# An involution and two ternary convolutions: three of seven neighbourhood columns transposed from SBUF instead of through DRAM

## The chip, the core and the metric

The kernel runs on one core of a Trainium2 chip. The metric is the device time of one execution in microseconds. Before the change three runs gave 2461.24, 2463.05 and 2464.96 us; the median is 2463.05 us. The profile comes from one further execution, whose span is 2469.9 us.

## The reference

The input x is float32 with 8 images, 256 channels and 56 x 56 positions. Two layers follow each other, and only the first is touched here.

```python
# layer 0, an involution with 7x7 taps and 16 groups of 16 channels
ker = einsum('bchw,oc->bohw', gn(x), w_reduce) + b_reduce        # 256 -> 64
ker = einsum('bchw,oc->bohw', ker, w_span) + b_span              # 64 -> 49*16
out = (ker.reshape(B, G, 1, 49, H, W) * patches(gn(x))).sum(axis=3)
x = x + out
# layer 1: two 3x3 convolutions with ternary weights, batch norms, relu
x = x + block(gn(x))
```

`gn` is a group norm with 32 groups. For each position and each group of 16 channels the involution makes 49 weights out of the 256 channels at that position, and sums the 7 x 7 neighbourhood (padded with zeros) with those weights. The ternary weights of the second layer depend on the mean, maximum and minimum of each whole weight tensor.

## The kernel before, in words

**Layout.** An image is worked on in four quarters (`NCQ`) of 64 channels. A quarter lies in SBUF as a tile `x` with 128 partitions: 64 channels of the upper half of the image (28 rows), then the same 64 channels of the lower half. The image is cut into tiles of 3 x 8 positions (`PY`, `PX`): ten tile rows (`TY`) in each half, the last with one row of positions, and seven tile columns (`TX`). The neighbourhood of a tile is 9 x 14 = 126 positions (`NQ`).

**The involution as matmuls.** For each tile and each group there is a matrix of 126 neighbours by 24 positions. TensorE makes these matrices from the reduced tensor `kr` and the slid weights `wl` (`generate`, line 606): 14 units for a quarter, each in one PSUM tile `pg` of two banks, that ACT (L631) and DVE (L636) move with the bias into the SBUF tile `a`. A unit has four to eight pixels' worth of matmuls; the ACT part of a unit comes first, and DVE's write to `a` waits for it. `apply_row` (line 646) then multiplies, for each tile row, the 126 neighbours by 128 channels (`q`) with the matrices: 28 small matmuls into one PSUM bank `pa` (L660). `pick_out` (line 666) takes the right half of each product out with ACT (L672) and DVE (L673) into `inv`, and POOL adds it to `x` in place (L676).

**The neighbourhoods.** `q` holds the neighbours on the partitions, so the normalised image must be transposed. `prep` (line 542) does this in strips of seven image rows: POOL normalises a strip and copies each tile column with its margin of three into `xn` (L565; three instructions for `PLACES`), TensorE transposes the seven columns into a PSUM tile `pt` (L571), ACT copies `pt` to `stg` (L574), and SP stores `stg` to a DRAM scratch `xtd` (L556, from the list `tasks`, two a row by `transfer`). `load_q` (line 592) reads for each tile row the 126 lines that it needs, 441 KB with all seven columns, four rows ahead (`NQB`, `prefetch`).

**The order of the work.** The main loop (lines 762 to 800) runs over 32 quarters of ten rows. A row issues, in this order: a store or load of x, two stores of strips, `apply_row`, the prefetch of a q, small statistics on DVE, `pick_out`, one or two units of the next quarter's `generate` (`PER_ROW`), and every row from the 24th of an image on one half step of `prep` for the next image (32 half steps, into row 15 of the next image). `pin` keeps each engine's instructions in the order of the text. Ahead of the loop stands a start that a scheduler orders: the first image's loads, `params` and `reduce`, `prep(0)`, the quantising of w1 and w2 (`quantize`, line 176, on DVE with one matmul for the sum, L201), and `generate` for the first quarter. The q buffers take their place in SBUF from the memory of the quantiser, so the first q loads wait for its last store.

**PSUM.** Eight banks: `ps_p` has three tiles of two banks, shared by `pg`, `pt`, the tiles `pk` of `reduce` (L524) and all small sums; `ps_a` has two banks for `pa`.

After the loop come two convolution phases (`conv_phase`) and a final pass. No line of theirs is changed.

Of the kernel before, what the change touches and what calls it, by code (L numbers as in the profile page):

```python
# [7 lines left out]
F32 = mybir.dt.float32  # L8
F32R = mybir.dt.float32r
AF = mybir.ActivationFunctionType  # L10
ALU = mybir.AluOpType
AX = mybir.AxisListType
PSUM = bass.MemoryType.PSUM
DRAM = bass.MemoryType.DRAM

P = 128
# [26 lines left out]

HQ = TY * PY + K - 1
RP = TX * P
SR = HH // 4
NSP = SR * QX

# [3 lines left out]

PER_ROW = (2, 1, 2, 1, 2, 1, 2, 1, 2, 0)
NQB = 4

NCB = 4
NC = NHW // NCB
# [14 lines left out]
@with_exitstack  # L74
def involution_tri_block_kernel(
    ctx: ExitStack, tc: tile.TileContext,
    x, w_red, b_red, w_line, b_tile, w1, w2, g1, b1, g2, b2, grp, ident, half, out,
):
    nc = tc.nc
    out = out.rearrange("b c h w -> b c (h w)")  # L80
# [348 lines left out]


    with ExitStack() as ph1:
        ps_p = ph1.enter_context(tc.tile_pool(name="ps_p", bufs=3, space=PSUM))
        ps_a = ph1.enter_context(tc.tile_pool(name="ps_a", bufs=2, space=PSUM))

        def ps_tile(name):
# [2 lines left out]
        def ps_flat(name):  # L438
            return ps_tile(name).rearrange("p a f -> p (a f)")

        xpool = ph1.enter_context(tc.tile_pool(name="xpool", bufs=2 * NCQ))
        fix = ph1.enter_context(tc.tile_pool(name="fix", bufs=1))
        work = ph1.enter_context(tc.tile_pool(name="work", bufs=2))

# [17 lines left out]
        def params(b):  # L462


            dst = small.tile([P, NCQ, 2], F32, tag="gn1", name=f"gn1_{b}")
            yield from group_norm_params(mvs.pop(b), dst, ps_flat, f"a{b}")
            ps = ps_flat(f"br_{b}")
            for c in range(NCQ):
                nc.vector.tensor_scalar(
                    wrn[:, c, :].rearrange("p (i r) -> p i r", i=2),  # L470
                    wr[:, c, :].unsqueeze(1).to_broadcast([P, 2, CR]),
                    dst[:, c, 0:1], None, ALU.mult)
                for i in range(2):
                    nc.tensor.matmul(ps[i * CR:(i + 1) * CR, :1], wr[:CH, c, :], dst[:CH, c, 1:2],
                                     start=(c == 0), stop=(c == NCQ - 1))
            prm[b] = dst
            yield
            nc.vector.tensor_tensor(brn, br, ps[:, :1], ALU.add)

        gst1, mvs = {}, {}  # L480
        prm, xs = {}, {}
        for c in range(NCQ):
            for j in range(2):
                load_x(0, c, j)
# [15 lines left out]
        bt = fixed([NQ, NCQ, GQ, NP], "bt", b_tile)  # L500
        kr = [fixed([P, PX, NT + (NE if py == 0 else 0)], f"kr{py}") for py in range(PY)]

        xn = fixed([P, TX, SR, QX], "xn")
        nc.gpsimd.memset(xn, 0.0)
        zero = xn.rearrange("p k r x -> p (k r x)")

        for d in (d for ds in xt_d for d in ds):
# [29 lines left out]

        PLACES = ((PAD, 0, PX), (0, PX - PAD, PAD), (PAD + PX, 0, PAD))  # L540

        def prep(b):

            for c in range(NCQ):
                d = xt_d[b % 2][c][:]

                def store(src, row, o=None, d=d):

                    n = src.shape[0]
                    if o is None:
                        src, to = src.rearrange("p k c -> p (k c)"), [[1, RP]]
                    else:
                        to = [[P, TX], [1, CH]]
                    nc.sync.dma_start(  # L556
                        bass.AP(d.tensor, d.offset + row * QX * RP + (o or 0), [[RP, n]] + to), src)

                for s in range(HH // SR):
                    xv = xs[b, c][:, s * SR * W:(s + 1) * SR * W].rearrange(  # L560
                        "p (r k j) -> p k r j", k=TX, j=PX)
                    for k, (x0, j0, n) in enumerate(PLACES):
                        to, fr = ((slice(0, TX), slice(0, TX)), (slice(1, TX), slice(0, TX - 1)),
                                  (slice(0, TX - 1), slice(1, TX)))[k]
                        nc.gpsimd.tensor_scalar(  # L565
                            xn[:, to, :, x0:x0 + n], xv[:, fr, :, j0:j0 + n],
                            prm[b][:, c, 0:1], prm[b][:, c, 1:2], ALU.mult, ALU.add)
                    yield
                    pt = ps_flat(f"pt_{b}_{c}_{s}")
                    for k in range(TX):  # L570
                        nc.tensor.transpose(pt[:NSP, k * P:(k + 1) * P],  # L571
                                            xn[:, k].rearrange("p r x -> p (r x)"), ident_sb)
                    stg = work.tile([P, TX, P], F32, tag="stg", name=f"stg_{b}_{c}_{s}")
                    nc.scalar.copy(stg[:NSP].rearrange("p k c -> p (k c)"), pt[:NSP, :RP])  # L574
                    tasks.append(lambda stg=stg, s=s: store(stg[:NSP], PAD + s * SR))

                    e = PAD * QX
                    if s == 0:
                        tasks.append(lambda stg=stg: store(stg[:e, :, CH:], PAD + HH, 0))
                    elif s == HH // SR - 1:  # L580
                        tasks.append(lambda stg=stg: store(stg[NSP - e:NSP, :, :CH], 0, CH))
                    yield
# [9 lines left out]
        def load_q(b, c, ty):  # L592

            q = qpool.tile([P, TX, P], F32, tag="q", name=f"q_{b}_{c}_{ty}")
            d = xt_d[b % 2][c][:]
            src = bass.AP(d.tensor, d.offset + PY * ty * QX * RP, [[RP, NQ], [1, RP]])
            nc.sync.dma_start(q[:NQ].rearrange("p k c -> p (k c)"), src)
            return q

        def views(a):  # L600

# [150 lines left out]
        quarters = [(b, c) for b in range(B) for c in range(NCQ)]  # L752


        X_AT = (0, 1, 4, 5, 7, 8, 10, 11)
        STRIPS_AT = 23
        for _ in range(NQB):
            prefetch()
        pin(start=True)
        last = None  # L760
        strips = iter(())
        for m, (b, c) in enumerate(quarters):
            a = a_next
            gen = iter(())
            if m + 1 < len(quarters):
                a_next = matrices(m + 1)
                gen = generate(*quarters[m + 1], a_next)
            more = b + 1 < B
            for ty in range(TY):
                r = c * TY + ty  # L770

                if last is not None and ty in (2, 3):
                    store_x1(*last, ty - 2)
                elif more and r in X_AT:
                    load_x(b + 1, X_AT.index(r) // 2, X_AT.index(r) % 2)
                transfer(2)

                row = apply_row(b, c, a, ty)
                prefetch()

                if more and r >= 20:
                    if r == 20:
                        norm = params(b + 1)
                    next(norm, None)
                if ty == 1 and last is not None:
                    gn2_stats(*last, TY)
                elif ty >= 2:
                    gn2_stats(b, c, ty - 1)
                if more and 4 <= r < 20:
                    gn1_stats(b + 1, (r - 4) // NCB, (r - 4) % NCB)  # L790
                pick_out(b, c, ty, *row)
                for _ in range(PER_ROW[ty]):
                    next(gen, None)
                if more and r == STRIPS_AT:
                    strips = prep(b + 1)
                next(strips, None)
                pin()
            for _ in gen:
                pass
# [107 lines left out]
```

## Time and profile before

| stretch, us | what runs | us | TensorE busy | TensorE clock | DMA share |
|---|---|---|---|---|---|
| 0 to 205 | start: first image, quantiser, first quarter's matrices | 205 | 63.1 | 0.64 | 0.40 |
| 206 to 1305 | loop over the quarters | 1099 | 908.6 | 0.92 | 0.72 |
| 1305 to 2220 | two convolution phases | 915 | 857.2 | 0.97, 0.96 | 0.34, 0.33 |
| 2220 to 2470 | final pass | 250 | 0 | 0.50 | 0.97 |

"TensorE busy" is the time in which at least one of its matmuls is under way. The clock is the share of full speed that the core was granted; 0.50 is the half clock in which TensorE stands when it has little to do. The DMA share is the mean busy share of the core's 16 DMA engines. In an idle column of the profile, "<-" names what ended a wait; "issue" stands where no semaphore ended it.

The largest DMA kinds of the loop are the q loads (441 KB each, 320 of them in the kernel), the strip stores (343 KB, 128), and the loads and stores of x (392 KB, 64 each).

### The profile page before, as it was taken

Reading aid. Unit: us, or ns where it says so; the run is one execution under the profiler, and the core shown is the slowest. Engines: PE = TensorE matmul, PEld = TensorE weight load, DVE = VectorE, ACT = ScalarE, POOL = GpSimd, SP = SyncE. Lnnn points to the kernel's source line nnn. Section 1 sums busy time; section 2 is a strip of 40 time slices with the busy share of each in tenths; the row PEclk is TensorE's granted clock in tenths of the full one; section 3 lists DMA queues with packets and bytes.
Section 4 is the critical chain, followed back from the end, with each engine's and each line's share of the span. In section 5 each row is a group of like instructions: output and inputs, shape, how many; then the busy total and the mean of one; then the engine's idle time right before and its main releaser. Section 6 shows DMA issues by size and latency. Waiting matters only on the chain.

```text
span 2469.9 us, 69728 instructions
## 1 busy us (share of the span) xinstructions
PE 1830.0 (74%) x30504; PEld 1700.9 (69%) x30504; DVE 1668.2 (68%) x2554; ACT 1171.8 (47%) x2084; POOL 381.7 (15%) x747
## 2 busy tenths in 40 slices
PE   3515878879787887878876999999499999980000
PEld 2315767768676776767766999999499999980000
DVE  4375656465555646455557999999499999974444
ACT  1202443445444353444433766676356667654433
POOL 1301232333323232332421000000000000000000
PEclk8557998899899898999997999999799999995555
DMA  5228587686858677585775332332423323329998
GB/s 173 89 115 271 167 253 207 209 236 196 255 168 249 202 222 231 176 257 172 234 220 194 130 136 107 117 146 83 183 89 142 116 107 143 123 84 429 428 429 373
DMA packets 127739, 485.44 MB, mean 197 GB/s; under 512 B 33102, under 2 KB 35532, under 8 KB 118732
## 3 DMA queue, kind: packets, MB, share of 16 engines
q1 hardware_dynamic: 121120, 440.03, 52.7%
q10 hardware_dynamic: 6316, 40.97, 4.0%
q8 instruction: 240, 3.93, 0.7%
q14 instruction: 63, 0.52, 0.1%
HBM read 315.76 MB, written 165.18 MB: 195 GB/s over the span
## 4 chain that ended last, share of the span: by engine, by line
PE 66%; DMA 13%; issue 10%; DVE 7%; POOL 2%; ACT 2%; ACTq 0%; SPq 0%; POOLq 0%; DVEq 0%
PE c L384 35%; PE pg L627 15%; PE pa L660 8%; PE pt L571 5%; DMA y1f<-y1d 4%; DMA out_y<-x1f 3%; PE pk L524 2%; DVE a L636 2%; POOL xn L565 1%; DVE x1f L845 1%; DMA x1f<-x1d 1%; ACT a L631 1%; DMA y2f<-y2d 1%; DMA w_w<-in_w 1%; DMA q<-xtd 1%
## 5 line engine op out<-in xcount | busy, mean ns | idle before, releaser
L384 PE MATMUL c<-pl,wq 128*128 128x392 f32 x4608 | 855.9, 348 | 50.3 <-ACT pl L290 32.4
L384 PEld LDWEIGHTS c<-pl,wq 128*128 128x128 f32 x4608 | 853.9, 189 | 52.1 <-ACT pl L290 33.2
L636 DVE TENSOR_TENSOR a<-pg,bt 126x756 f32<-126x756 f32 (+3 forms) x640 | 393.1, 657 | 296.1 <-ACT a L631 256.3
L627 PE MATMUL pg<-kr,wl 64*126 64x140 f32 (+1 forms) x6144 | 485.5, 306 | 78.1 <-issue 54.5
L627 PEld LDWEIGHTS pg<-kr,wl 64*126 64x126 f32 x6144 | 420.7, 207 | 103.1 <-issue 79.5
L660 PE MATMUL pa<-a,q 126*32 126x48 f32 x17920 | 282.9, 212 | 151.6 <-issue 84.7
L660 PEld LDWEIGHTS pa<-a,q 126*32 126x32 f32 x17920 | 233.5, 115 | 208.2 <-issue 168.4
L631 ACT ACTIVATE a<-pg,bt 126x126 f32<-126x126 f32 x768 | 242.7, 475 | 242.7 <-PE pg L627 242.7
L676 POOL TENSOR_TENSOR x<-x,inv 128x168 f32<-128x168 f32 x320 | 166.0, 519 | 800.0 <-DVE inv L673 783.6
L672 ACT ACTIVATE inv<-pa,half_sb 128x168 f32<-128x168 f32 x320 | 126.1, 394 | 298.2 <-PE pa L660 283.4
L673 DVE SCALAR_TENSOR_TENSOR inv<-pa,half_sb,inv 128x168 f32<-128x168 f32 x320 | 118.7, 371 | 195.4 <-ACT inv L672 193.7
L290 ACT CAST pl<-r 128x812 fp32r<-128x812 f32 x192 | 162.5, 867 | 153.9 <-DVE r L285 136.7
L565 POOL TENSOR_SCALAR xn<-x,gn 128x126 f32<-128x126 f32 (+1 forms) x384 | 205.3, 558 | 63.1 <-DMA xtd<-xn 34.0
L347 ACT ACTIVATE dummy<-y,nc 128x1568 f32<-128x1568 f32 x128 | 205.4, 1605 | 15.6 <-DVE y L370 14.3
L291 DVE TENSOR_TENSOR pl<-r,pl 128x812 fp32r<-128x812 f32 x192 | 186.9, 1002 | 30.3 <-ACT pl L290 29.4
L574 ACT COPY stg<-pt 98x896 f32<-98x896 f32 x128 | 117.0, 914 | 159.0 <-PE pt L571 114.6
L571 PE MATMUL pt<-ident_sb,xn 128*98 128x128 f32 x896 | 148.0, 308 | 48.2 <-POOL xn L565 39.3
L571 PEld LDWEIGHTS pt<-ident_sb,xn 128*98 128x98 f32 x896 | 105.8, 141 | 79.4 <-POOL xn L565 55.3
L135 DVE BATCH_NORM_STATS2 st<-x 128x6 f32<-128x392 f32 x256 | 138.1, 556 | 10.3 <-DMA x<-in_x 9.9
L271 POOL MEMSET xp<- 128x116 f32 x32 | 6.3, 196 | 817.0 <-DVE a L285 816.9
L826 ACT ACTIVATE xp<-raw,bi_bn,sc_bn 128x392 f32<-128x392 f32 (+1 forms) x128 | 84.8, 720 | 71.7 <-DVE a L285 57.1
L816 ACT ACTIVATE xp<-raw,gn 128x392 f32<-128x392 f32 (+1 forms) x128 | 85.2, 721 | 56.7 <-DVE a L285 50.9
(127 smaller groups left out, 1362.0 us busy)
## 6 DMA issues: line engine op xcount, KB each, us to landing
q<-xtd SPq DMA_DIRECT2D x320, 441.0 KB
xtd<-stg SPq DMA_DIRECT2D x128, 343.0 KB
raw<-x1d SPq DMA_DIRECT2D x32, 812.0 KB
raw<-y1d SPq DMA_DIRECT2D x32, 812.0 KB
x<-in_x SPq DMA_DIRECT2D x64, 392.0 KB
x1d<-x SPq DMA_DIRECT2D x64, 392.0 KB
y1d<-y SPq DMA_DIRECT2D x32, 784.0 KB
y2d<-y SPq DMA_DIRECT2D x32, 784.0 KB
```

The lines of the kernel that those rows point to most:

```text
L135: nc.vector.bn_stats(st[:, j, :], xt[:, j * NC:(j + 1) * NC])
L290: nc.scalar.copy(hi, r)
L291: nc.vector.tensor_tensor(lo, r, hi.bitcast(F32), ALU.subtract)
L347: nc.scalar.activation(dummy, y[:, to], f, bias=shift[:, to:to + 1], accum_out=stats[:, to, j, n:n + 1])
L384: nc.tensor.matmul(ps[:, to, :NM], wq[:, k, t, dx, to * P:(to + 1) * P], part[:, t, :, dx:dx + W], start=(c == 0), stop=(c == last))
L565: nc.gpsimd.tensor_scalar(xn[:, to, :, x0:x0 + n], xv[:, fr, :, j0:j0 + n], prm[b][:, c, 0:1], prm[b][:, c, 1:2], ALU.mult, ALU.add)
L571: nc.tensor.transpose(pt[:NSP, k * P:(k + 1) * P], xn[:, k].rearrange("p r x -> p (r x)"), ident_sb)
L627: nc.tensor.matmul(dst, wl[rows, c, gp, o:o + NQ], kr[py][rows, px, :], start=True, stop=True)
L631: nc.scalar.activation(whole[:, g0 + i, p0 + j], ps[:NQ, i, j * nt:(j + 1) * nt], AF.Identity, bias=bt[:, c, g0 + i, p0 + j:p0 + j + 1])
L636: nc.vector.tensor_tensor(dst[:, g0:g0 + 2, p0:p0 + nv].rearrange("q g p t -> q g t p"), ps[:NQ, :, t0 * nv:t1 * nv].rearrange("q i (t p) ...
L660: nc.tensor.matmul(ps[o:o + 32, k * 2 * n:(k + 1) * 2 * n], q[:NQ, k, o:o + 32], av[:, t + k, g * 2 * n:(g + 1) * 2 * n], start=True, stop ...
L676: nc.gpsimd.tensor_tensor(xv, xv, iv.rearrange("p t (y x) -> p y t x", x=PX), ALU.add)
```

## The change

Tile columns 0 to 3 (`NK` = 4) keep the way through DRAM. Columns 4 to 6 (`NX` = 3) get their neighbourhoods on the chip:

- `surround(b, c)` builds for one quarter a tile `xe` (3 columns x 34 rows x 14 positions on 128 partitions, two of them, zeroed once): POOL normalises the quarter in four parts of seven rows, and in one more part the three rows above and below each half. Those six rows come from a new input `x_around` by a load of 168 KB; `side` turns the shift of the norm off where the rows lie outside the image. One part is issued in every second row (even `ty`), for the next quarter.
- `transpose_q(b, c, ty)` transposes the three columns of a tile row into a PSUM bank `pt` and lets ACT copy them into the free part of that row's `q`. In the loop it stands right after `apply_row` and the prefetch, for the row two ahead (`QLEAD`).
- `xn`, `stg`, the scratch `xtd` and the DMAs on them shrink from seven columns to four.
- PSUM: `ps_p` goes from three tiles to two; the strips' transposes leave it and share two new banks `pt` of the pool `ps_a` with `transpose_q`.
- `x` has seven buffers instead of eight, and the load of an image's fourth quarter moves from rows 10 and 11 to rows 14 and 15.

```diff
+NK = 4
+NX = TX - NK
 HQ = TY * PY + K - 1
-RP = TX * P
+RP = NK * P
+QLEAD = 2
...
-        ps_p = ph1.enter_context(tc.tile_pool(name="ps_p", bufs=3, space=PSUM))
+        ps_p = ph1.enter_context(tc.tile_pool(name="ps_p", bufs=2, space=PSUM))
...
-        xpool = ph1.enter_context(tc.tile_pool(name="xpool", bufs=2 * NCQ))
+        xpool = ph1.enter_context(tc.tile_pool(name="xpool", bufs=2 * NCQ - 1))
...
-        xn = fixed([P, TX, SR, QX], "xn")
+        xn = fixed([P, NK, SR, QX], "xn")
+        xe = [fixed([P, NX, HQ, QX], f"xe{i}") for i in range(2)]
...
+        def surround(b, c):
+            dst, p = xe[c % 2], prm[b]
+            around = work.tile([P, 2, PAD * W], F32, tag="xa", name=f"xa_{b}_{c}")
+            nc.sync.dma_start(around.rearrange("p s f -> p (s f)"), x_around[b, c])
+            for part in (0, 1, None, 2, 3):
+                if part is None:
+                    for j, r0 in enumerate((0, PAD + HH)):
+                        spread(dst[:, :, r0:r0 + PAD], around[:, j], NK, NX,
+                               p[:, c, 0:1], prm_edge[b][:, j, c:c + 1])
+                else:
+                    r0 = part * SR
+                    spread(dst[:, :, PAD + r0:PAD + r0 + SR], xs[b, c][:, r0 * W:(r0 + SR) * W],
+                           NK, NX, p[:, c, 0:1], p[:, c, 1:2])
+                yield
...
-                    pt = ps_flat(f"pt_{b}_{c}_{s}")
-                    for k in range(TX):
+                    pt = ps_a.tile([P, 512], F32, tag="pt", name=f"pt_{b}_{c}_{s}")
+                    for k in range(NK):
...
-            nc.sync.dma_start(q[:NQ].rearrange("p k c -> p (k c)"), src)
+            nc.sync.dma_start(q[:NQ, :NK].rearrange("p k c -> p (k c)"), src)
             return q
+
+        def transpose_q(b, c, ty):
+            pt = ps_a.tile([P, 512], F32, tag="pt", name=f"ptq_{b}_{c}_{ty}")
+            for k in range(NX):
+                nc.tensor.transpose(
+                    pt[:NQ, k * P:(k + 1) * P],
+                    xe[c % 2][:, k, PY * ty:PY * ty + QY].rearrange("p r x -> p (r x)"), ident_sb)
+            nc.scalar.copy(loads[b, c, ty][:NQ, NK:].rearrange("p k c -> p (k c)"),
+                           pt[:NQ, :NX * P])
...
-        X_AT = (0, 1, 4, 5, 7, 8, 10, 11)
+        X_AT = (0, 1, 4, 5, 7, 8, 14, 15)
         STRIPS_AT = 23
         for _ in range(NQB):
             prefetch()
+        for _ in surround(0, 0):
+            pass
+        rows = [(b, c, ty) for b, c in quarters for ty in range(TY)]
+        for k in rows[:QLEAD]:
+            transpose_q(*k)
...
                 row = apply_row(b, c, a, ty)
                 prefetch()
+                if m * TY + ty + QLEAD < len(rows):
+                    transpose_q(*rows[m * TY + ty + QLEAD])
...
                 next(strips, None)
+                if ty % 2 == 0 and m + 1 < len(quarters):
+                    next(around)
                 pin()
```

`spread` is the old three-instruction copy of `prep` as a function with the columns as arguments; `edge` holds the two shifts for the border rows (two small DVE instructions an image).

## Prediction

> **What bounds the kernel now.** I read the page's slices first, then the busy times by stretch, then TensorE's waits inside the stretch that the change touches, and last the order of time around one wait.
>
> ```profile
> 0.00:205.00 205.00, 63.14 (x429) 48.06 (x433) 99.40 (x119) 27.67 (x49) 27.97 (x57) 0.64 0.40 141
> 206.00:1305.00 1099.00, 908.63 (x25427) 796.91 (x25417) 626.27 (x1356) 475.22 (x1231) 340.71 (x655) 0.92 0.72 216
> 1305.00:1760.00 455.00, 429.08 (x2314) 428.12 (x2308) 415.66 (x518) 285.37 (x383) 10.03 (x20) 0.97 0.34 128
> ```
>
> Columns: stretch, length, busy us and instructions of PE, PEld, DVE, ACT, POOL, then clock, DMA share, GB/s. The change lies in the start (0 to 205) and in the loop over quarters (206 to 1305); from 1305 on nothing is edited. In the loop TensorE is busy 909 of 1099 us, DVE 626, ACT 475, POOL 341. So TensorE sets the end, and its idle 190 us is the thing to explain:
>
> ```profile
> PE pa L660 <- issue: 84.7, 51, 3.7
> PE pg L627 <- issue: 54.5, 24, 5.4
> PE br L474 <- DVE gn L157: 12.8, 7, 2.0
> PE pa L660 <- DVE a L636: 12.3, 18, 1.3
> PE pt L571 <- issue: 8.3, 6, 3.3
> ```
>
> 147.5 of the 190 us are "issue": no semaphore held TensorE. TensorE's own order of time shows where:
>
> ```profile
> 610.23 0.38 PE L571 MATMUL pt<-ident_sb,xn 128*98 128x128 f32 x2 [1.11 <-issue]
> 610.54 0.80 PE L660 MATMUL pa<-a,q 126*32 126x48 f32 x56
> 611.27 1.15 PE L627 MATMUL pg<-kr,wl 64*126 64x126 f32 x16
> 612.35 0.79 PE L660 MATMUL pa<-a,q 126*32 126x48 f32 x53
> 614.38 0.28 PE L660 MATMUL pa<-a,q 126*32 126x48 f32 x3 [1.24 <-issue]
> ```
>
> It stops inside one row's matmuls, 53 of 56 done. Between the two stops lie 2+56+16+53 = 127 matmuls with as many weight loads, 254 instructions. The queue list says what comes in such lots:
>
> ```profile
> q8 instruction: 240, 3.93, 0.7%
> ```
>
> 240 packets of 16 KB for some 61,000 TensorE instructions: 256 instructions a packet. Counting TensorE's records, every long stop of the loop stands at the same place modulo 256, and ends about 1.4 us after a q8 packet has landed. So TensorE runs out of instructions. Of the loop's 200 block boundaries 81 have a gap over 0.35 us, 165.6 us from start to start (the view's 147.5 leaves out the modelled tail of the matmul before each gap).
>
> What delays the packet is the data that SP has in flight. For each of the 200 I set the time from the start of the block before to the packet's start against the bytes that SP had issued and that had not moved: correlation 0.79, slope 2.6 us per MB. Under 300 KB outstanding (53 blocks) the mean stop was 0.1 us, 300 to 500 KB (40) 0.30, 500 to 800 KB (50) 0.83, 800 to 1200 KB (33) 1.50, above (24) 2.63.
>
> A long stop costs twice, because the clock falls after it:
>
> ```profile
> 682.60:684.60 2.00, 0.24 (x9) 0.11 (x8) 2.00 (x5) 0.73 (x2) 0.54 (x1) 1.00 0.91 238
> 685.00:689.00 4.00, 4.00 (x80) 3.82 (x71) 1.08 (x3) 1.65 (x5) 0.54 (x1) 0.57 0.63 185
> ```
>
> A stop of 2.0 us with DMA 0.91 busy, and then 4 us at clock 0.57. Start-to-start distances in half-clock stretches against the same pairs elsewhere give an excess of 72 us over the loop. The loop's 1099 us are thus about 809 of matmuls at full clock, 72 of slow clock, 166 of missing instructions and some 50 of other waits.
>
> In the start one wait matters:
>
> ```profile
> 102.91 0.16 DVE L203 TENSOR_SCALAR mean_w<-sum_w 128x1 f32<-128x1 f32 x1 [55.48 <-PE sum_w L201]
> ```
>
> The quantizer's mean waits 55.5 us for a small matmul that stands in TensorE's queue behind all sixteen strips of `prep(0)`.
>
> **What the Trainium skill says.** "Runtime: NRT & Kernel Launch", Instruction fetch mechanics: instructions come in 16 KiB blocks of 256 over the engine's own DMA queue, and this is mostly hidden. The trace agrees on the block and not on the hiding (166 us). "DMA: Bandwidth & Descriptors", Queues, rings and completion order: each DMA engine takes its queues in turn, packet by packet, so a fetch should wait for little; here its delay grows with SP's backlog (2.6 us per MB), and I go by the measurement. "TensorE: Matmul & The Clock Gate", Part 1: after an idle window of about 3.4 us the clock halves; the trace has it after a stop of 2.0 us. "PSUM — Partial Sum Buffer", The four PSUM rules: neither GpSimd nor DMA reads PSUM, which is why each new transpose costs an ACT copy.
>
> **The change part by part.** (1) TensorE's transposes. Neighbours in one strip start 0.117 us apart at full clock, and the last of a strip holds the next instruction back 0.206 (means of the start-to-start distances of `pt`). Added: three for each row, 2x0.117+0.206 = 0.44 us, for 318 rows in the loop 140 us. Removed: three of seven for each of 112 strips, 0.35 us, 39 us. Sum +101 us, all on the engine that sets the end.
>
> (2) Instruction fetch. Per image SP moves now 40x441 + 16x343 + 8x73.5 + 16x392 KB = 30.0 MB, afterwards 40x252 + 16x196 + 8x42 + 16x392 + 4x168 = 20.5 MB. The DMA share should fall from 0.72 to about 0.50, and one q load from 441 to 252 KB. Backlog falls with both the load and the size of one transfer; I take half. The five groups, moved down by half (500-800 becomes 250-400 and so on; stops of 0.1, 0.1, 0.2, 0.5, 1.1 us), give 60 us of stops in place of 166: -106. At 0.7 of the backlog it is -55, at 0.3 -125. The 72 more transposes per image add half a block per image: nothing.
>
> (3) Clock. Stops of 2 us and more bring the half clock and nearly vanish in (2): 72 becomes 22, -50 (ends -20 and -65).
>
> (4) PSUM. `ps_p` has two buffers in place of three, for pg, pk and small sums alone; strips and rows share two banks of their own. A unit of pg is free 1.0 to 2.0 us after its last matmul (ACT, then DVE, L631, L636). Set against the start of the unit after next in the trace before, two buffers would have held TensorE 18 us in all, mostly the second unit of a row. In the new order each such interval contains one more 0.44 us of transposes, while the ACT copy stands ahead of `inv` and of the row's units and shifts their release by about as much. Fewer fetch stops take slack away: +25 (ends 10 and 80).
>
> (5) ACT. The row's copy is 126x384; the stg copy of 896 elements took 0.91 us and `inv` of 168 took 0.39, so about 0.5. 40 of these less 16x0.35 per image are +14 us on 62 busy of 142; behind the copy wait `inv`, then DVE's and POOL's part of the row, which has two `pa` banks and three `inv` buffers of room. Nothing beyond (4).
>
> (6) POOL. xn of 392 elements took 0.72 us and of 126 0.48, 0.36 + 0.9 ns an element: a strip falls from 1.7 to 1.4, a `surround` part costs 1.3, the border part 2.4. Per image 21 of x sums + 23 + 31 = 75 us in 135, strips in odd rows and parts in even ones. Consumers are a row or more away: nothing.
>
> (7) Loads. `x` of the fourth quarter moves to rows 14 and 15, behind the store that frees its buffer (rows 12 and 13); SP may stand a microsecond there, in front of q loads that run four rows ahead. Its statistics come at row 16. Nothing; at worst 2 us per image. The `x_around` loads, 168 KB, are in (2).
>
> (8) Start. Compiled, the changed kernel has the quantizer's sum matmul directly behind the first strip, because strips no longer take `ps_p`. The mean then comes at 47.5, and the quantizer's DVE part (103 to 127) ends near 72. Now the strips bind: they run from 55.6, 3.13 us each (POOL 1.21 before the first transpose, PE 1.92); with four columns 0.97 + 1.16 = 2.13. The fifteenth is through at 55.6+14x2.13 = 85.4, two pg units at half clock (2.07 each) follow, and ACT can issue the first load of w2 at about 90, not 133.9. The six loads were in at 147.8; mixed with ACT's pg work they take a little longer, to 105 or 108. What follows (57 us to the first `pa` at 204.9) is unchanged. Gain 40 us (ends 15 and 45). The first block's `surround` runs while POOL waits for the zeroing DMAs (34 us) and hides.
>
> Sum: +101 -106 -50 +25 in the loop = -30; start -40; together -70. The profiled execution has 2469.9, so its counterpart should show about 2400; the timed median, 2463.05, becomes 2393.
>
> **The rivals.** Slower: the fetch delay does not follow the data volume, but comes from the packet's own latency (1.1 us on the way, 1.4 after it). Then (2) and (3) give nothing, the loop gains 126 us and the start gives back 40: 2549. It decides from where (2) and (3) together bring less than 86 of their 238 us. The correlation speaks against it; that blocks under 300 KB still wait about a microsecond for their packet speaks for a floor. Faster still: with DMA at half load stops go to 15 us and slow clock to 5: 2463 -218 +126 -40 = 2331. PSUM turn: two buffers hold TensorE 80 us, not 25: 2448; the lag of 2.0 us against 2.2 us to the unit after next says that it is close. Start unmoved, since another wait replaces the sum's (the w2 load still behind ACT's queue): 2433.
>
> **How the numbers follow.** My forecast (2360 to 2425) 0.50; faster still 0.17; PSUM turn 0.13; start unmoved 0.11; slower 0.09. The range 2325 to 2455 leaves out the slower case and the tails. A difference under 0.2% can't be told from none here. Faster 0.88, same 0.03, slower 0.09.
>
> **What would show it.** DMA share of the loop near 0.5; "issue" in front of pa and pg near 50 us, not 148; mean clock of the loop 0.96 or more; PE busy in the loop hardly changed (transposes in, slow clock out); "PE pg <- DVE a" up from nothing to 15 to 40 us; first `pa` near 165, not 205; q landing earlier; `mean_w` no longer waiting 55 us. I am wrong if "issue" stays above 110 us, if pg waits for DVE over 70, or if the first `pa` stands where it stood.

## The result and the profile after

The changed kernel takes 2426.2 us (median of 4 runs, 2421.8 to 2433.7) against 2464.0 us beside it (4 runs): ratio 0.984, 95% interval 0.981 to 0.988. The gain is 38 us where about 70 were forecast. The profiled run spans 2421.5 us against 2469.9.

Busy times by stretch of the kernel after (columns as before: PE, PEld, DVE, ACT, POOL, clock, DMA share, GB/s); the first is the start, the second the loop over quarters:

```profile
0.00:184.00 184.00, 53.07 (x382) 41.05 (x382) 100.23 (x121) 23.22 (x51) 46.19 (x77) 0.65 0.39 136
184.00:1255.40 1071.40, 974.17 (x26086) 813.75 (x26086) 627.91 (x1369) 568.62 (x1549) 533.22 (x1212) 0.97 0.52 152
```

The start fell from 204.9 to 184.0 us (-21). The loop, from the first `pa` to the last, fell from 1100.1 to 1071.4 (-28.7). In the loop TensorE is busy 66 us longer, at 0.97 of full clock instead of 0.92, with the DMA share at 0.52 instead of 0.72. TensorE's waits in the loop after:

```profile
PE pg L671 <- DVE a L680: 24.5, 15, 2.1
PE pa L704 <- issue: 16.2, 16, 2.1
PE br L478 <- DVE gn L161: 14.6, 7, 2.1
PE pg L671 <- issue: 14.4, 18, 1.7
PE pa L704 <- DVE a L680: 10.2, 24, 0.8
PE pk L538 <- DVE a L680: 8.3, 7, 1.2
```

"issue", the time without instructions, is 33 us (16.2, 14.4 and 2.4 before `ptq`) instead of 147.5. In its place pg and pk now wait for DVE's copies, 24.5 and 8.3 us, which were not in the view before. The number of instruction packets hardly moved:

```profile
q8 instruction: 244, 4.00, 0.7%
```

So the packets come earlier; there are not fewer. In TensorE's order of time one stop still cuts a row's matmuls, 32 of 56 done, and the next row then passes without one:

```profile
608.48 0.55 PE L704 MATMUL pa<-a,q 126*32 126x48 f32 x32
610.13 0.46 PE L704 MATMUL pa<-a,q 126*32 126x48 f32 x24 [1.10 <-issue]
610.52 0.55 PE L638 MATMUL ptq<-ident_sb,xe 128*126 128x128 f32 x3
611.00 1.86 PE L671 MATMUL pg<-kr,wl 64*126 64x126 f32 x28
612.79 0.64 PE L605 MATMUL pt<-ident_sb,xn 128*98 128x128 f32 x4
613.37 0.80 PE L704 MATMUL pa<-a,q 126*32 126x48 f32 x56
614.10 0.55 PE L638 MATMUL ptq<-ident_sb,xe 128*126 128x128 f32 x3
```

And the quantizer's mean comes at 46, no longer at 103:

```profile
45.95 0.15 DVE L207 TENSOR_SCALAR mean_w<-sum_w 128x1 f32<-128x1 f32 x1
```

From the trace records I made the same budget of the loop for every kernel. "Matmuls" are the start-to-start distances at full clock (up to 0.42 us each, so a very short wait hides in them), "stops" the gaps over 0.35 us at the block boundaries, "slow clock" the excess of the half-clock stretches, "rest" what is left of the loop. All in us; backlog is the mean of the bytes that SP had issued and that had not moved.

| kernel | first `pa` | loop | matmuls | stops | slow clock | rest | backlog, KB |
|---|---|---|---|---|---|---|---|
| before | 204.9 | 1100.1 | 809 | 166 | 72 | 53 | 635 |
| after | 184.0 | 1071.4 | 932 | 45 | 23 | 71 | 253 |
| e1_before_q4: loads of 4 columns | 203.5 | 997.2 | 811 | 100 | 36 | 50 | 353 |
| e6_before_q4_s4: loads and stores of 4 | 202.9 | 981.7 | 807 | 74 | 40 | 60 | 293 |
| e3_before_psum: PSUM shared anew | 183.0 | 1148.1 | 821 | 148 | 72 | 107 | 613 |
| e10_before_nqb3: one load buffer fewer | 202.4 | 1107.9 | 802 | 113 | 70 | 122 | 590 |
| e2_after_q7: after, 169 KB more a row | 182.5 | 1108.4 | 932 | 82 | 24 | 71 | 377 |
| e5_after_wide: after, loads of 441 KB | 182.5 | 1149.1 | 931 | 93 | 46 | 79 | 433 |
| e4_start_act: after, first strips on ACT | 162.0 | 1070.4 | 933 | 39 | 26 | 72 | 251 |
| e7_act_quarters: e4, x in quarters | 161.7 | 1069.5 | 933 | 40 | 26 | 71 | 236 |
| e8_act_nk5: e4, two columns by TensorE | 166.0 | 1077.2 | 909 | 54 | 30 | 85 | 353 |
| e9_act_psum3: e4, PSUM a third way | 159.0 | 1108.1 | 891 | 6 | 24 | 187 | 230 |
| e11_act_nqb3: e4, three load buffers | 163.6 | 1067.2 | 929 | 37 | 27 | 75 | 252 |
| e12_act_xn2: e11, two xn buffers | 156.3 | 1064.0 | 930 | 36 | 24 | 74 | 253 |

The rows are single profiled executions. Where a verdict rests on a difference of a few us, the timed ratio stands beside it below.

### The profile page after: what moved, and what is told of

The parts are those of the page before. It is cut to its first block, busy times and chain, and to the rows that moved or that the text cites. A ratio compares the mean times of both kernels' runs of the same rounds, so it can differ in the third digit from the quotient of the medians.

```text
span 2421.5 us, 72092 instructions
## 1 busy us (share of the span) xinstructions
PE 1885.9 (78%) x31080; PEld 1711.2 (71%) x31080; DVE 1671.0 (69%) x2570; ACT 1261.0 (52%) x2404; POOL 592.9 (24%) x1325
## 4 chain that ended last, share of the span: by engine, by line
PE 41%; DMA 10%; DVE 2%; ACT 1%; issue 1%; SPq 0%; POOL 0%; ACTq 0%; DVEq 0%
PE c L388 35%; DMA y1f<-y1d 3%; PE pg L671 3%; DMA out_y<-x1f 2%; DMA x1f<-x1d 2%; PE pa L704 2%; DVE x1f L899 1%; PE ptq L638 1%; DMA y2f<-y2d 1%; DMA y1d<-y 1%; DMA wq<-wqd 1%; PE pk L538 0%; PE pt L605 0%; ACT a L675 0%; DVE a L680 0%
## 5 line engine op out<-in xcount | busy, mean ns | idle before, releaser
L671 PE MATMUL pg<-kr,wl 64*126 64x140 f32 (+1 forms) x6144 | 460.9, 293 | 56.8 <-DVE a L680 32.5
L671 PEld LDWEIGHTS pg<-kr,wl 64*126 64x126 f32 x6144 | 394.8, 194 | 112.0 <-issue 70.3
L704 PE MATMUL pa<-a,q 126*32 126x48 f32 x17920 | 270.4, 208 | 71.5 <-DMA q<-xtd 44.5
L641 ACT COPY q<-ptq 126x384 f32<-126x384 f32 x320 | 153.0, 478 | 314.0 <-issue 171.0
L704 PEld LDWEIGHTS pa<-a,q 126*32 126x32 f32 x17920 | 221.7, 111 | 128.5 <-issue 89.4
L561 POOL TENSOR_SCALAR xn<-x,gn 128x224 f32<-128x224 f32 (+2 forms) x384 | 184.2, 500 | 29.1 <-PE pt L605 18.5
L638 PE MATMUL ptq<-ident_sb,xe 128*126 128x128 f32 x960 | 178.6, 296 | 9.4 <-ACT stg L608 7.0
L561 POOL TENSOR_SCALAR xe<-x,gn 128x168 f32<-128x168 f32 (+2 forms) x384 | 160.3, 437 | 19.9 <-DVE gn L161 19.9
L608 ACT COPY stg<-pt 98x512 f32<-98x512 f32 x128 | 79.9, 624 | 122.0 <-PE pt L605 61.6
L638 PEld LDWEIGHTS ptq<-ident_sb,xe 128*126 128x126 f32 x960 | 101.3, 143 | 29.7 <-ACT stg L608 7.2
```

Of the source, the lines that this page charges most:

```text
L561: nc.gpsimd.tensor_scalar(dst[:, i - d - k0:f - d - k0, :, x0:x0 + n], v[:, i:f, :, j0:j0 + n], scale, bias, ALU.mult, ALU.add)
L638: nc.tensor.transpose(pt[:NQ, k * P:(k + 1) * P], xe[c % 2][:, k, PY * ty:PY * ty + QY].rearrange("p r x -> p (r x)"), ident_sb)
L641: nc.scalar.copy(loads[b, c, ty][:NQ, NK:].rearrange("p k c -> p (k c)"), pt[:NQ, :NX * P])
L671: nc.tensor.matmul(dst, wl[rows, c, gp, o:o + NQ], kr[py][rows, px, :], start=True, stop=True)
L704: nc.tensor.matmul(ps[o:o + 32, k * 2 * n:(k + 1) * 2 * n], q[:NQ, k, o:o + 32], av[:, t + k, g * 2 * n:(g + 1) * 2 * n], start=True, stop ...
```

## The experiments

**Is it the volume? Before with lighter loads.**

```diff
-    src = bass.AP(d.tensor, d.offset + PY * ty * QX * RP, [[RP, NQ], [1, RP]])
-    nc.sync.dma_start(q[:NQ].rearrange("p k c -> p (k c)"), src)
+    src = bass.AP(d.tensor, d.offset + PY * ty * QX * RP, [[RP, NQ], [1, 4 * P]])
+    nc.sync.dma_start(q[:NQ, :4].rearrange("p k c -> p (k c)"), src)
...
-    q[:NQ, k, o:o + 32],
+    q[:NQ, k % 4, o:o + 32],
```

> The kernel before, with one edit: each load of a neighbourhood brings only four of its seven tile columns (252 KB instead of 441 KB a row of tiles), and the products read those four columns in turn; the matmuls, copies and transposes are the same in number and shape, but the output comes from the wrong columns. Fetch theory (the stops of TensorE at the ends of its instruction blocks grow with the data that SP's queue has outstanding): the stops in the rows' loop fall from 166 us to 40 to 60, the half-clock excess from 72 to about 22, and the loop from 1100 to 930 to 1000 us at unchanged matmul time; whole kernel 2300 to 2350 us. Rival (the stops come from the latency or the number of packets of the fetch itself, and the change moved them in another way, for instance by the extra TensorE work between them): stops within 20 us of 166, loop and whole kernel within 20 us of before.

2366.6 us, ratio 0.959 (0.955 to 0.962). With TensorE's work unchanged the loop lost 103 us, 66 of stops and 36 of slow clock. The rival is out: the data that SP moves do delay the instruction packets. But 100 us of stops remained, not 40 to 60, and the kernel stayed above the 2300 to 2350 that were expected.

**The stores too.**

```diff
-    src, to = src.rearrange("p k c -> p (k c)"), [[1, RP]]
+    src, to = src[:, :4].rearrange("p k c -> p (k c)"), [[1, 4 * P]]
...
-    to = [[P, TX], [1, CH]]
+    src, to = src[:, :4], [[P, 4], [1, CH]]
```

> The kernel before with loads of four columns of seven and, besides, stores of four columns of seven: SP moves the volume of the kernel after, while TensorE, ACT and POOL do the work of the kernel before; the output comes from the wrong columns. Loads of four columns alone had left 100 us of stops and 36 us of half-clock excess at a mean backlog of 353 KB. Volume theory: the backlog comes to about 250 KB, the stops to 45 to 70 us, the half-clock excess to 20 to 30 us, the loop to 935 to 970 us. Rival (the longer rows with TensorE's transposes give the rest of the fall to 45 us): stops stay at 80 to 100 us, the loop at 975 to 997 us.

2351.1 us, ratio 0.955 (0.952 to 0.957). SP's queue moved 357 MB in all, where the kernel after moves 361. Stops 74, slow clock 40, loop 982: the stops lie between the two theories, the loop where the rival put it. The loop's line:

```profile
205.00:1184.00 979.00, 868.70 (x25358) 762.47 (x25354) 622.36 (x1356) 470.78 (x1230) 338.81 (x655) 0.95 0.54 161
```

At the volume of the kernel after (DMA share 0.54 against 0.52) the stops and the slow clock together still cost 114 us, where the kernel after has 68. Volume alone gives -118 us of loop; the last 46 us of the fall in stops and slow clock need something else of the change.

**The volume of before in the kernel after, first try.**

```diff
+    more = qpool.tile([P, 336], F32, tag="more", bufs=2, name=f"more_{b}_{c}_{ty}")
+    src = bass.AP(d.tensor, d.offset + PY * ty * QX * RP, [[RP, NQ], [1, 336]])
+    nc.sync.dma_start(more[:NQ], src)
```

> The kernel after, with one addition: behind each row's loads SP brings 126 x 336 numbers (169 KB) more from the same columns into a tile that nothing reads, so that a row loads 421 KB again against 441 KB before. TensorE's work is untouched. Fetch theory: the stops come back from 45 us to 120 to 170, the half-clock excess from 23 to 50 to 75, and the loop grows from 1071 to 1170 to 1220 us, so that the kernel is slower than the one before, at 2520 to 2570 us. Rival (the loads' volume has nothing to do with the stops): loop within 20 us of 1071, kernel within 20 us of 2426.

2471.8 us, ratio 1.001 (0.998 to 1.004): the gain is gone, but the loop grew by 37 us, not by 100 to 150, and the slow clock did not come back at all. One reason is in SP's own waits:

```profile
SPq L634 <- DMA more<-xtd: 30.1, 35, 1.9
```

The added load has two buffers, and SP stood 30 us until the one before last had landed. That holds the backlog down (377 KB), so this run does not carry the volume as the kernel before does.

**Second try: the load of the kernel before in the kernel after.**

```diff
+    n = TX if ty < TY - 1 else NK
-    src = bass.AP(d.tensor, d.offset + PY * ty * QX * RP, [[RP, NQ], [1, RP]])
-    nc.sync.dma_start(q[:NQ, :NK].rearrange("p k c -> p (k c)"), src)
+    src = bass.AP(d.tensor, d.offset + PY * ty * QX * RP, [[RP, NQ], [1, n * P]])
+    nc.sync.dma_start(q[:NQ, :n].rearrange("p k c -> p (k c)"), src)
```

> The kernel after, with one edit: in nine rows of ten the load brings 126 x 896 numbers (441 KB, packets of 3584 B, as in the kernel before) instead of 126 x 512; the last three columns are overwritten by the TensorE transposes' copies, so the result is the same. TensorE's work is untouched. The run with 169 KB more in a load of its own had shown the stops back at 82 us only, with a mean backlog on SP's queue of 377 KB against 635 KB in the kernel before, and its extra load had waited for its own buffer (22.8 us of SP waits), which held the backlog down. Backlog theory: without that wait the mean backlog comes to 450 to 600 KB, the stops to 90 to 150 us, the half-clock excess to 30 to 60 us, the loop to 1115 to 1200 us. Rival (the row with transposes on TensorE is less open to the stops whatever the volume, since blocks with slow transposes last longer): stops at most 90 us, half-clock excess at most 28 us, loop 1095 to 1120 us. A copy of the transposes that now waits for a load would show as ACT waiting for DMA q.

2498.1 us, ratio 1.014 (1.011 to 1.017): with the loads at 441 KB the change is a loss. Stops 93, slow clock 46, loop 1149 lie where the backlog theory put them; the backlog, 433 KB, came just below its range. Part of the 78 us may be a wait that the edit itself brings, in ACT's waits:

```profile
ACT q L642 <- DMA q<-xtd: 70.9, 44, 3.2
```

The copy of the transposes now waits for the load that it overwrites; but the rest of the budget rose by only 8 us, so little of it reached TensorE.

Together with before, e6 and after this makes a square. Its second row has all of the change, and its "full volume" is 417 MB on SP's queue in e5 against 440 in before:

| | full volume | volume of after |
|---|---|---|
| without TensorE's transposes | 1100 (stops 166, slow clock 72) | 982 (74, 40) |
| with them, PSUM and all else of the change | 1149 (93, 46) | 1071 (45, 23) |

The volume is worth 78 to 118 us. The rest of the change, mainly the transposes and the new PSUM, costs 49 to 90 net, although it lengthens the matmuls by over 120: it wins back 46 to 99 us of stops and slow clock. Two numbers hint at how. The shortest blocks of 256 instructions grew: the tenth percentile of a block's time is 3.0 us in before and e6, 3.6 in after and 3.7 in e5. And at the same backlog of 500 to 800 KB the mean stop is 0.73 to 0.97 us in before, e3, e1 and e6, but 0.48 to 0.71 in e4, e5, e2 and after. The two ranges nearly touch, and e10, which has no transposes either, comes to about 0.5, so this is a hint and no more. A block that lasts longer leaves more time for the next packet. The longer rows also spread nearly the same bytes over more time (635 to 433 KB of backlog from before to e5). A third candidate is the new waits for PSUM buffers, since a wait can hide a stop: alone, in e3, they come with 18 us fewer stops. How much is due to each of the three is argued, not shown.

**The new sharing of PSUM alone.**

```diff
-    ps_p = ph1.enter_context(tc.tile_pool(name="ps_p", bufs=3, space=PSUM))
+    ps_p = ph1.enter_context(tc.tile_pool(name="ps_p", bufs=2, space=PSUM))
...
-    pt = ps_flat(f"pt_{b}_{c}_{s}")
+    pt = ps_a.tile([P, 2, 512], F32, tag="pt", bufs=1,
+                   name=f"pt_{b}_{c}_{s}").rearrange("p a f -> p (a f)")
```

> The kernel before with the new sharing of PSUM alone: the general buffers are two, and the strips at the start are transposed into one two-bank tile of their own; the three columns are not transposed by TensorE and the loads are whole. If the sharing alone moves the start: the matmul of the quantiser's sum no longer stands behind the strips' turns, mean_w comes near 46 instead of behind the strips, and the first matmul of a product comes 15 to 30 us before 204.9; in the loop two buffers add 15 to 30 us of waits of pg and pk for the copies of the products, mainly behind DVE's a. Sum: within 15 us of before. If the loop's waits do not come from the buffers, the kernel is 15 to 30 us faster than before; if the start's gain came from the lighter loads, the first matmul of a product stays within 5 us of 204.9 and the kernel is 15 to 30 us slower.

2502.9 us, ratio 1.014 (1.010 to 1.017). The first `pa` came at 183.0, 22 us earlier: the sharing alone gives all of the start's gain, and the kernel after with its narrower strips (184.0) has no more. The loop rose by 48 us, more than expected. Its waits:

```profile
PE pg L628 <- DVE a L637: 29.5, 36, 2.1
...
PE pk L524 <- DVE a L637: 8.2, 7, 1.2
...
PE pg L628 <- DVE brn L478: 3.7, 7, 0.5
```

41 us of waits that the kernel before does not have. So two general buffers cost some 40 us where the stops stay about as they are (166 to 148 us).

**Why the start gained 21 us and not 40.** From the kernel after in order of time, POOL's normalising of the second, third and fourth strip, and a DVE line between them:

```profile
53.95 4.52 POOL L561 TENSOR_SCALAR xn<-x,gn 128x224 f32<-128x224 f32 x3 [7.46 <-issue]
...
59.78 11.03 POOL L561 TENSOR_SCALAR xn<-x,gn 128x224 f32<-128x224 f32 x3 [1.32 <-PE pt L605]
...
68.94 1.74 DVE L239 SCALAR_TENSOR_TENSOR u_w<-g_w,w_w 128x1536 f32<-128x1536 f32 x1
...
72.14 1.33 POOL L561 TENSOR_SCALAR xn<-x,gn 128x224 f32<-128x224 f32 x3 [1.32 <-PE pt L605]
```

The same three instructions took 4.5, 11.0 and then 1.3 us, as they do in every later strip. The longest lies beside the quantizer's back-to-back DVE instructions with two inputs in SBUF; the last of these ends at 70.7, and POOL is free at 70.8. The one of 4.5 us begins beside two such instructions, until 55.4, and goes on beside shorter ones with one input. The edit gives the strips of the first image to ACT:

```diff
-    nc.gpsimd.tensor_scalar(
-        dst[:, i - d - k0:f - d - k0, :, x0:x0 + n], v[:, i:f, :, j0:j0 + n],
-        scale, bias, ALU.mult, ALU.add)
+    if act:
+        nc.scalar.activation(to, fr, AF.Identity, bias=bias, scale=scale)
+    else:
+        nc.gpsimd.tensor_scalar(to, fr, scale, bias, ALU.mult, ALU.add)
...
-    prm[b][:, c, 0:1], prm[b][:, c, 1:2])
+    prm[b][:, c, 0:1], prm[b][:, c, 1:2], act=b == 0)
```

> The kernel after, with one edit: the first image's strips are normalised by ACT and not by POOL (the same numbers, other engine). Theory: in the start of the kernel after, two of POOL's normalising triples took 4.5 and 11.0 us instead of 1.3 while DVE ran the quantiser, and the strips then went on at 2.65 us each where 2.13 was forecast; ACT does not slow down beside DVE, so the triples keep one length throughout, the first matmul of a product comes 10 to 30 us before 184, and the kernel is at 2396 to 2416 us, the loop unchanged. Rival (the strips' end is not what the first product waits for; the w2 loads or ACT's other work take their place): first matmul of a product within 5 us of 184, kernel within 8 us of 2426.

2406.8 us, ratio 0.977 (0.973 to 0.981). The first `pa` came at 162.0, 22 us earlier, with the loop unchanged (1070.4). ACT's triples keep their length beside the same DVE work:

```profile
43.28 1.27 ACT L563 ACTIVATE xn<-x,gn 128x224 f32<-128x224 f32 x3
...
49.79 1.27 ACT L563 ACTIVATE xn<-x,gn 128x224 f32<-128x224 f32 x3
...
52.72 1.27 ACT L563 ACTIVATE xn<-x,gn 128x224 f32<-128x224 f32 x3
```

"SBUF — State Buffer" of the Trainium skill, Who interferes with whom, says that a DVE instruction with two SBUF inputs contends with a GpSimd instruction that reads SBUF, and that the later of the two is blocked. The trace of the kernel after agrees, and adds the size: two POOL instructions that take 0.42 us in later strips took 5.07 us each, through three DVE instructions in a row, and their triple eight times its usual time.

The edit changes more than the stretch, though. ACT takes up the second strip at 43.28, where POOL began it only at 53.95, after its two reductions for the quantizer. By the two traces about 11 of the 22 us come from this earlier beginning; the two triples had cost about 13, and ACT's longer period, 2.93 us a strip instead of 2.65, takes some back.

**Further runs around the best version.** The loads of x in quarters:

```diff
-    X_AT = (0, 1, 4, 5, 7, 8, 14, 15)
+    X_AT = (0, 0, 1, 4, 5, 6, 7, 8, 9, 10, 11, 11, 14, 14, 15, 16)
...
-    elif more and r in X_AT:
-        load_x(b + 1, X_AT.index(r) // 2, X_AT.index(r) % 2)
+    elif more:
+        for i in range(len(X_AT)):
+            if X_AT[i] == r:
+                load_x(b + 1, i // 4, i % 4, 4)
```

> The kernel after with the first image's strips normalised by ACT, and the loads of the next image's x in sixteen pieces of 196 KB over rows 0 to 16 instead of eight of 392 KB over rows 0 to 15: the same volume, smaller bursts. Backlog theory: the stops after rows 0 to 16 fall, from 39 us in all to 25 to 35, the loop from 1070 to 1055 to 1066 us, the kernel to 2390 to 2402 us. Rival (the bursts do not matter): loop within 4 us of 1070, kernel within 5 us of 2407.

2398.2 us, ratio 0.975 (0.971 to 0.979); loop 1069.5, stops 40. The rival holds for the loop: these bursts do not matter.

Two columns by TensorE instead of three (the strip's five columns in two PSUM tiles):

```diff
-    NK = 4
+    NK = 5
```

> The kernel after with the first image's strips normalised by ACT, and two columns of seven transposed by TensorE instead of three, five by DRAM; a strip's five columns go through two PSUM tiles with a copy each. By the sums of the prediction: about 47 us fewer of transposes from SBUF, about 16 us more of strips' transposes, while the load grows from 252 to 315 KB: stops from 39 to 55 to 80 us, half-clock excess from 26 to 28 to 40 us. Loop 1055 to 1090 us (1070 with three columns), kernel 2390 to 2425 us: near flat. If stops and clock follow the volume steeply, as from 252 to 441 KB, the loop is above 1090 us; if the transposes are what the loop pays for, it is below 1055 us.

2410.7 us, ratio 0.978 (0.975 to 0.981). The matmuls fell by 24 us; stops, slow clock and rest gave 32 back. Between two and three columns the loop is flat.

PSUM a third way:

```diff
-    ps_p = ph1.enter_context(tc.tile_pool(name="ps_p", bufs=2, space=PSUM))
-    ps_a = ph1.enter_context(tc.tile_pool(name="ps_a", bufs=2, space=PSUM))
+    ps_p = ph1.enter_context(tc.tile_pool(name="ps_p", bufs=3, space=PSUM))
+    ps_a = ph1.enter_context(tc.tile_pool(name="ps_a", bufs=1, space=PSUM))
```

> The kernel after with the first image's strips normalised by ACT and PSUM shared out a third way: three general buffers again, one bank for the rows' product pa and one for the transposes (both had two). If the 18 us by which the other waits of the rows' loop grew (53 to 71 us; TensorE's pg, pa and pk behind DVE's a: 43 us) come from the general buffers being two, the loop falls from 1070 by 15 to 30 us, to 1040 to 1055, unless pa with one bank waits for the row before: that can happen where a row has no pg behind it, once in ten rows, at most 0.7 us each or 22 us, and would show as pa waiting for DVE inv. Start: the strips take turns on one bank, 0 to 10 us later than 162. Kernel 2385 to 2415 us. Rival (the waits belong to DVE being behind, whatever the buffers): loop within 5 us of 1070.

2435.9 us, ratio 0.988 (0.986 to 0.989): by the ratios 1.1% slower than e4 with two banks each, a wrong expectation. The waits behind DVE's a are gone, but one line replaces them:

```profile
PE pa L706 <- DVE inv L719: 101.9, 149, 1.9
```

I had counted one wait in ten rows; it is one in two. The run shows two things besides. The stops fell to 6 us at an almost equal backlog (230 KB): while TensorE waits for inv, the next block arrives. A wait elsewhere hides a stop. And pg's matmuls took 369 us of distances, against 395 in e4: some 26 us of that kernel's "matmuls" may be short waits for PSUM buffers or instructions. The kernel before, with three general buffers, has 392, so the number of buffers does not explain them.

One load buffer fewer, in before and in e4:

```diff
-    NQB = 4
+    NQB = 3
```

> The kernel before with three buffers for the loads instead of four: same volume, same instructions, one load of 441 KB fewer that can stand in SP's queue. Backlog theory (the fetch waits behind what is outstanding, about 2.1 to 2.6 us per MB, not behind the volume as such): mean backlog from 635 to 300 to 500 KB, stops from 166 to 100 to 140 us, half-clock excess from 72 to 40 to 60 us, loop 1020 to 1080 us, unless TensorE's pa begins to wait for the loads, which would show as pa waiting for DMA q. Rival (volume and share of the DMA engines alone decide): stops 155 to 175 us, loop within 10 us of 1100.

2482.9 us, ratio 1.005 (1.003 to 1.007). The stops fell to 113 us as expected, but the mean backlog hardly (590 KB), the slow clock stayed at 70, and TensorE waited for the loads themselves:

```profile
PE pa L660 <- DMA q<-xtd: 59.4, 43, 4.0
```

So this run doesn't separate backlog from volume; as in e9, a new wait of TensorE goes with fewer stops.

> The kernel after with the first image's strips normalised by ACT and three buffers for the loads instead of four. Backlog theory: mean backlog from 251 to 150 to 220 KB, stops from 39 to 25 to 36 us, half-clock excess from 26 to 18 to 26 us, loop 1052 to 1068 us, kernel 2390 to 2405 us. Against it: the copy of a row's transposes, two rows ahead, and pa may wait for loads that are issued a row later: if pa's or ACT's waits for DMA q grow by more than 15 us, the loop is at or above 1070.

2398.1 us, ratio 0.972 (0.969 to 0.974): loop 1067, 3 us less than e4, backlog 252 KB as in e4. The backlog theory's fall did not come; neither did a wait for the loads. At the smaller volume three buffers are enough, which leaves SBUF for one more edit:

```diff
-    xn = fixed([P, NK, SR, QX], "xn")
+    xns = [fixed([P, NK, SR, QX], f"xn{i}") for i in range(2)]
...
+    xn = xns[s % 2]
```

> The kernel after with the first image's strips normalised by ACT, three buffers for the loads, and the strips' input xn in two buffers, so that the next strip is normalised while TensorE transposes this one. With one buffer and ACT the strips follow each other at 2.93 us (1.27 us on ACT, 1.32 to hand over and transpose, the rest waits), and the first product came as much earlier (22 us) as the last strip. With two, ACT is the limit: 1.27 us and a copy of 0.58 us, 1.9 to 2.1 us a strip, so fourteen strips save 11 to 14 us; first matmul of a product at 149 to 153 us (163.6 with one buffer), loop within 6 us of 1067, kernel 2382 to 2390 us. If another chain (SP's stores of the strips, the quantiser of w2) takes over, the first product comes less than 6 us earlier and the kernel stays at 2393 to 2400 us.

2391.7 us, ratio 0.970 (0.968 to 0.972): the best version, by the ratios 1.5% below the kernel after. The strips were through at 74 us instead of 98.7, but the first `pa` came only 7 us earlier (156.3), between the 149 to 153 that were expected and the less than 6 us of the alternative. The chain that took over is visible in ACT's order of time: the quantized w1 goes out, and ACT's next copy then waits for a strip's store behind it, with the loads of w2 behind the copy.

```profile
72.70 0.34 ACTq L240 DMA_DIRECT2D wqd<-u_w  x1
...
87.45 1.07 ACT L612 COPY stg<-pt 98x512 f32<-98x512 f32 x2 [14.50 <-DMA xtd<-stg]
...
88.05 0.36 ACTq L194 DMA_DIRECT2D w_w<-in_w  x1
```

## Why the prediction was right in sign and too large

**(1) Transposes: 123 us, not 101.** The `ptq` took 148.5 us where 140 were summed and the strips gave back 36 where 39 were; `pa`, `pg` and `pk` became some 12 us longer between them. The last is a cost that the sum did not have; that it is short waits is a guess from e9.

**(2) Instruction fetch: -121 us, forecast -106.** The size was right, the reason half right. The prediction put all of it down to SP's volume; at that volume alone (e6) the stops stay at 74 us, and the full volume with the transposes (e5) already has only 93. It didn't see that the rest of the change, most likely its own step (1) above all, leaves the fetch more time.

**(3) Clock: -49 us, forecast -50.** Right, with the same qualification: 40 us of slow clock at e6, 23 with the transposes.

**(4) PSUM: the rest of the loop rose by 18 us, forecast 25.** Named correctly, pg and pk behind DVE's a: 33 us of new waits. Alone it costs more (e3).

**(5) to (7)**: right in that no wait of the loop's TensorE names ACT's copies, POOL or a load. The copy measured 478 ns, against 0.5 us.

The loop thus came to -28.7 us where the steps had -30. That the sum fits this well is partly luck: the transposes cost 22 us more than forecast, and the fetch gave 15 and PSUM 7 better. **The step that failed is (8), the start: -21 us, forecast -40.** The sum's matmul did move directly behind the first strip, and the mean came at 46.0 (forecast 47.5). But the strips were taken at 2.13 us each from 55.6, with the fifteenth through at 85.4 and the first load of w2 at 90. In the trace the fifteenth was through at 103.9. About 13 us of that are the two stretched POOL triples: the prediction moved POOL's strips beside the quantizer's DVE work and took both durations from stretches in which they had run apart. A further 7 us are the period over 13 strips, 2.65 instead of 2.13 us: POOL 1.33 and then 1.32 until TensorE has read `xn`, where the sum had 0.97 and 1.16; 1.7 us came back, since the first began at 53.95. And the first load of w2 came 10 us after the fifteenth strip, not 5, for a reason that the working didn't have, seen in the kernel after:

```profile
98.64 0.34 ACTq L240 DMA_DIRECT2D wqd<-u_w  x1
...
114.05 0.58 ACT L608 COPY stg<-pt 98x512 f32<-98x512 f32 x1 [12.19 <-DMA xtd<-stg]
...
114.24 0.33 ACTq L194 DMA_DIRECT2D w_w<-in_w  x1
```

The store of the quantized w1 is 4608 KB, in packets of 36 KB. The strips' stores of 196 KB issued behind it move in packets of 2 KB. From 103 to 111 us the two queues moved about as many packets, 84 and 69, but 2952 and 138 KB, so the first of the stores was through only when w1 nearly was. ACT's copy needs that store's buffer, and the loads of w2 are queued on ACT behind the copy.

With the strips on ACT (e4) the first `pa` came at 162.0, near the 165 forecast, but by another course: the strips begin earlier than the sum had them and follow each other more slowly, and the w1 store holds ACT up there too:

```profile
87.84 0.58 ACT L610 COPY stg<-pt 98x512 f32<-98x512 f32 x1 [8.05 <-DMA xtd<-stg]
```

**The rivals.** "Slower" is refuted by e1 and e6, though e5, at 2498, shows that the kernel would have been slower had the volume not fallen. "Faster still" didn't come: 45 us of stops remain, and some 33 of them stand at the ends of the 42 blocks of 204 that began with over 500 KB outstanding. The mean backlog fell, but such bursts are left. "PSUM turn": 18, not 80. "Start unmoved": half true, and for the kind of reason that it named, the load of w2 behind ACT's queue. Of the signs two failed: the first `pa` near 165, and "PE busy hardly changed": it rose 66 us, since 123 us of matmuls came in and 49 of slow clock went. Whether q lands earlier was not measured.

## What to carry to other kernels

When TensorE runs out of instructions, count the bytes that stand in the queues (shown here by lighter loads and stores) and the time that a block of instructions lasts (argued here): both bear on whether the next block is there, and a wait elsewhere can hide the stop. Work moved from DMA to TensorE pays here only because the traffic fell; the same transposes at nearly the old traffic lost 1.4%. When a change moves work beside other work, take its duration from a stretch in which they really ran side by side, and look for a large store in large packets that the moved work's small stores have to share the DMA engines with.

## What the runs showed of the hardware

Three POOL instructions reading SBUF stretched from 1.3 to 11.0 us together beside back-to-back two-input DVE instructions, while ACT's kept 1.27. The delay of an instruction packet grew by 2.1 to 2.6 us per MB outstanding on SP's queue in before, e1, e2, e3, e5, e6 and after alike, from 0.55 to 0.9 us at none. And a single 4608 KB store in packets of 36 KB held up another queue's 196 KB stores in packets of 2 KB, and with them ACT, by 8.1 us (e4), 12.2 (after) and 14.5 (e12).
